# Pair products on one core: 31 rows of sixteen by difference, three TensorE turns a tile, ScalarE's queue for the head loads and the last two stores

## The chip, the cores and the metric

The kernel runs on one core of one Trainium2 chip. The metric is the device time of one execution in microseconds (us). Before the change it is 1284.42 us, the median of 3 runs that lie between 1284.36 and 1284.61.

## The reference

For 4096 batch rows, 32 fields and an embedding of 64, every pair of fields i < j is multiplied, the second field after a product with the 64x64 matrix W:

```python
vid = jnp.einsum('bfd,de->bfe', x, W)          # x: (4096, 32, 64)
idx_i, idx_j = jnp.triu_indices(32, k=1)       # 496 pairs
return x[:, idx_i, :] * vid[:, idx_j, :]       # (4096, 496, 64), float32
```

The input has 33.6 MB, the output 520 MB.

## The kernel before

The host lays the embedding (64) of two halves of the batch on the 128 partitions and cuts the rest of the batch into 16 tiles of 128 rows. A field of a tile is thus 128 partitions x 128 floats, called a unit below (512 bytes on a partition, 64 KB in all). A tile has 32 units of input and 496 units of output. The memory `mem` has 446 units; inputs and results share it.

For each tile TensorE multiplies eight blocks of four fields by `w2` (W twice on a diagonal) into the eight banks of `vid`, which fill the PSUM. VectorE multiplies fields of `mem` by fields of `vid`, one instruction for many pairs (line 247), and writes the results into `mem`. `SLOTS` is a table of 68 pieces of the output in order, each with its length in units and its place in `mem`; slot k is stored by one DMA, here called s0 to s67, when its last product is done (line 259). A slot's place is that of older slots or of spent inputs, so the first product into it waits until the store that still reads there has landed. `CUTS` are further points at which a product is split.

All DMAs are issued by SyncE, so all are in SP's queue, in program order. `HEAD` are the loads at the start: half of tile 0 (`x0`), `w`, and 176 units more in three DMAs. Two `STRETCHES` of 160 units, tiles 6 to 10 and 11 to 15, are loaded behind slots 24 and 45 (`LOAD_BEHIND`), three DMAs each. After each group of loads the next store is held until the last load but one has landed (`held`). A DMA of 128 partitions is 128 rows, one for each partition, so that each of the 16 DMA engines moves eight rows of it.

ScalarE computes nothing: it waits for loads and for VectorE's reads of the banks and then lets TensorE go with the semaphore `go`, once for each half of the banks, so twice a tile. `by_block` orders the pairs of a tile: the pairs within fields 0 to 15, the 16x16 between the halves, and the pairs within fields 16 to 31. At the end SyncE waits for the last stores, clears the semaphores and waits for s67.

Of the kernel before, what the change touches and what calls it, by code (L numbers as in the profile page):

```python
# [12 lines left out]
P = 128  # L13
# [13 lines left out]
HEAD = range(6), [(302, 128), (0, 32), (430, 16)]  # L27
STRETCHES = [
    (range(6, 11), [(286, 128), (414, 16), (430, 16)]),
    (range(11, 16), [(32, 128), (16, 16), (0, 16)]),  # L30
]

# [12 lines left out]
]  # L45
CUTS = {
    3: (46,), 6: (24,), 11: (64,), 17: (110,), 21: (6,), 28: (24,), 36: (112,), 40: (120,),
    47: (14,), 52: (30,), 53: (24,), 54: (16,), 55: (30,), 57: (48,), 59: (112,), 61: (32,),
    64: (112,), 65: (118,), 66: (32,),
}  # L50
LOAD_BEHIND = [24, 45]
# [6 lines left out]
def by_block():  # L58


    def within(lo):
        yield "step", lo, 2, 1, 0
        for k in range(2):
            yield "step", lo, 4, 2, k
        for i in (lo, lo + 8):
            yield "row", i + 4, i, 4, 4
        yield "row", lo + 8, lo, 8, 8

    yield from within(0)
    yield "row", 16, 0, 16, 16  # L70
    yield from within(16)


def products(at, ends):


    for kind, a, b, c, d in by_block():
        if kind == "row":
            rows, n, i0, di, j0, dj = c, d, b, 0, a, 1
        else:  # L80
            rows, n, i0, di, j0, dj = 16 // b, c, a, b, a + c + d, b
        r = k = 0
        while r < rows:
            room = ends[bisect_right(ends, at)] - at
            if k or room < n:
                m, w = 1, min(n - k, room)
            else:
                m, w = min(rows - r, room // n), n
            yield at, m, w, i0 + r * di + k, di, j0 + r * dj, dj
            at += m * w  # L90
            if k + w == n:
                r, k = r + m, 0
            else:
                k += w


HALF = F // 2
# [20 lines left out]

def build(nc, x0, x, w, out):
# [16 lines left out]
    seen_sp = set()  # L136
    sp_dve = 0

    def sp_wait_dve(n):
        nonlocal sp_dve  # L140
        if n > sp_dve:
            nc.sync.wait_ge(dve, n)  # L142
            sp_dve = n

    def sp_wait(s):
        if s.num not in seen_sp:
            nc.sync.wait_ge(s, 16)
            seen_sp.add(s.num)

    def load(dst, src, name, fields):  # L150
        s = sem(name)
        nc.sync.dma_start(dst, src).then_inc(s, 16)  # L152
        for t, f in fields:
            loaded[t, f] = s
        return s


    load(mem[:, PLACE[0] : PLACE[0] + HALF, :], x0[:, :HALF, :], "x0", [(0, f) for f in range(HALF)])
    ws = load(w2, w, "w", [])

    at = 0

    def stretch(tiles, runs, name):
        nonlocal at
        made = []
        for r, (lo, n) in enumerate(runs):
            for k in track.stores(lo, lo + n):
                sp_wait(stored[k])
            sp_wait_dve(track.reads(lo, lo + n))
            made.append(load(mem[:, lo : lo + n, :], x[:, at : at + n, :], f"{name}{r}", fields(tiles, lo, n)))  # L170
            for u in range(lo, lo + n):
                track.store[u] = None
                track.read[u] = 0
            at += n
        return made

    held = stretch(*HEAD, "h")[-2]

    for tiles, first, step in WALKS:
        with nc.tensor.Fori(0, len(tiles)) as k:
            for b in range(F // BANK):
                if b % (HALF // BANK) == 0:
                    nc.tensor.wait_ge(go, 1)
                    nc.tensor.sem_inc(go, -1)  # L186
                nc.tensor.matmul(  # L187
                    vid[:, b * BANK : b * BANK + BANK, :],
                    lhsT=w2,
                    rhs=mem[:, bass.ds(k * step + (first + b * BANK), BANK), :],  # L190
                    start=True,
                    stop=True,
                ).then_inc(pe, 1)
# [3 lines left out]
    rank = {}  # L197
    done = 0
    bank_read = [0] * (F // BANK)
    seen_act, seen_dve = set(), set()  # L200
    act_dve = dve_pe = dve_dve = 0
# [4 lines left out]
    for t in range(NT):  # L206
        place = PLACE[t]
        for b in range(0, F // BANK, HALF // BANK):
            for s in [ws, *(loaded[t, f] for f in range(b * BANK, b * BANK + HALF))]:
                if s.num not in seen_act:  # L210
                    nc.scalar.wait_ge(s, 16)
                    seen_act.add(s.num)
            read = max(bank_read[b : b + HALF // BANK])
            if read > act_dve:
                nc.scalar.wait_ge(dve, read)
                act_dve = read
            nc.scalar.sem_inc(go, 1)

        xt = mem[:, place : place + F, :]
        for pos, m, n, i, di, j, dj in products(t * NP, ends):  # L220
            begin = STARTS[slot]
            size, lo = SLOTS[slot]
            u = lo + pos - begin
            o = mem[:, u : u + m * n, :]
            if m == 1:
                left = xt[:, i : i + n, :]
                right = vid[:, j : j + 1, :].to_broadcast([P, n, C])
            else:
                o = o.rearrange("p (m w) c -> p m w c", m=m)
                right = vid[:, j : j + (m - 1) * dj + 1 : dj, :].unsqueeze(2).to_broadcast([P, m, n, C])  # L230
                if di == 0:
                    left = xt[:, i : i + n, :].unsqueeze(1).to_broadcast([P, m, n, C])
                else:
                    left = xt.rearrange("p (m d) c -> p m d c", d=di)[:, i // di : i // di + m, i % di : i % di + n, :]
            last = j + (m - 1) * dj
            need = t * (F // BANK) + last // BANK + 1
            if need > dve_pe:
                nc.vector.wait_ge(pe, need)
                dve_pe = need
            for s in track.stores(u, u + m * n):  # L240
                if s not in seen_dve:
                    nc.vector.wait_ge(stored[s], 16)  # L242
                    seen_dve.add(s)
            if track.reads(u, u + m * n) > dve_dve:
                dve_dve = track.reads(u, u + m * n)
                nc.vector.wait_ge(dve, dve_dve)  # L246
            nc.vector.tensor_tensor(o, left, right, MULT).then_inc(dve, 1)  # L247
            done += 1
            for r in range(m):
                for f in range(i + r * di, i + r * di + n):  # L250
                    track.read[place + f] = done
                bank_read[(j + r * dj) // BANK] = done
            if pos + m * n == begin + size:
                if held is not None:
                    sp_wait(held)
                    held = None
                sp_wait_dve(done)
                s = sem(f"s{slot}")
                nc.sync.dma_start(out[:, begin : begin + size, :], mem[:, lo : lo + size, :]).then_inc(s, 16)  # L259
                stored.append(s)  # L260
                for u in range(lo, lo + size):
                    track.store[u] = slot
                slot += 1
                if waiting and waiting[0] == slot:
                    waiting.pop(0)
                    held = stretch(*stretches.pop(0), f"g{slot}_")[-2]
# [3 lines left out]
    for k, s in enumerate(landed):  # L270
        if k not in seen_dve:
            sp_wait(s)
    numbers = sorted(s.num for s in sems)
    assert numbers == list(range(numbers[0], numbers[-1] + 1)) and final.num == numbers[-1]
    nc.sync.sem_clear(range(numbers[0], numbers[-1]))
# [4 lines left out]
def pairs():  # L280
    for _, m, n, i, di, j, dj in products(0, [NP]):
        for r in range(m):
            for k in range(n):
                yield i + r * di + k, j + r * dj
# [34 lines left out]
```

## Time and profile before

| | |
|---|---|
| median of 3 runs | 1284.42 us |
| the profiled execution: time, span | 1284.54 us, 1283.2 us |
| VectorE (DVE) busy | 1080.3 us, 292 products |
| TensorE busy, weight loads | 182.4 us, 71.2 us |
| DMA queue q1 | 99.9% of 16 engines over the span |
| DMA bytes | 33.62 MB read from HBM, 520.09 MB written, 432 GB/s |
| granted TensorE clock, mean | 0.567 |

The shares of the busy time are of the whole span. For the DMA the share is the time that packets took, as a part of what 16 engines have in the span. The profiled execution is 0.12 us above the median of the runs.

### The profile page before, as it was taken

To read this page: it belongs to the slowest core of one execution; us is meant where nothing else is said; L and a number is where in the kernel's file an instruction comes from. 1 tells how busy PE (TensorE), PEld (TensorE's weight loads), DVE (VectorE), ACT (ScalarE), POOL (GpSimd) and SP (SyncE) were. 2 spreads that over 40 slices of the span, in tenths; PEclk is the share of its full clock that TensorE was granted. 3 is DMA by queue.
4 is the path that set the end of the run, shared out by engine and by line. 5 is a ranking of instruction groups with operands and counts; after the bars stand their busy time and mean duration, and the time that the engine had idled before them with its cause. 6 is when DMAs were issued, how large, how long until landed. Compare 5 with 4: busy or idle time off the path is not lost.

```text
span 1283.2 us, 1172 instructions
## 1 busy us (share of the span) xinstructions
PE 182.4 (14%) x256; PEld 71.2 (6%) x256; DVE 1080.3 (84%) x292; POOL 0.2 (0%) x4
## 2 busy tenths in 40 slices
PE   4011040304020021021111201002112030111000
PEld 1000010101000010000000000000001010000000
DVE  5798999999996556989999998483898999899971
POOL 0000000000000000000000000000000000000000
PEclk7656565755555565555565656556556565665555
DMA  9999999999999999999999999999999999999999
GB/s 415 424 441 437 426 440 429 437 421 439 445 427 433 417 437 445 423 443 421 435 424 447 442 427 417 435 419 453 427 433 425 454 429 425 425 444 437 427 425 409
DMA packets 11380, 553.75 MB, mean 432 GB/s; under 512 B 1264, under 2 KB 1392, under 8 KB 1392
## 3 DMA queue, kind: packets, MB, share of 16 engines
q1 hardware_dynamic: 11376, 553.72, 99.9%
q14 instruction: 4, 0.03, 0.0%
HBM read 33.62 MB, written 520.09 MB: 432 GB/s over the span
## 4 chain that ended last, share of the span: by engine, by line
DVE 50%; DMA 40%; another core or an unknown queue 4%; issue 3%; SPq 0%; DVEq 0%
DVE mem L247 50%; DMA out_dram<-mem 38%; DMA mem<-in_r_x_dram 2%; SPq L152 0%; SPq L259 0%; DVEq L242 0%; SPq L142 0%; DVEq L246 0%
## 5 line engine op out<-in xcount | busy, mean ns | idle before, releaser
L247 DVE TENSOR_TENSOR mem<-mem,vid 128x1024 f32<-128x1024 f32 (+11 forms) x292 | 1080.3, 3771 | 175.4 <-DMA out_dram<-mem 144.1
L187 PE MATMUL vid<-mem,w 128*128 (+1 forms) x256 | 182.4, 880 | 1002.4 <-PEq L186 1002.4
L187 PEld LDWEIGHTS vid<-mem,w 128*128 128x128 f32 x256 | 71.2, 292 | 1112.7 <-issue 1112.7
L292 POOL MEMSET const-bfloat16-1.0<- 128x1 bf16 x1 | 0.1, 102 | 0.0
L292 POOL MEMSET const-uint8-127<- 128x1 uint8 x1 | 0.1, 102 | 0.0
L292 POOL MEMSET const-float32-0.0<- 128x1 f32 x1 | 0.1, 99 | 0.2 <-issue 0.2
L292 POOL MEMSET const-float32-1.0<- 128x1 f32 x1 | 0.1, 99 | 0.0
## 6 DMA issues: line engine op xcount, KB each, us to landing
out_dram<-mem SPq DMA_DIRECT2D x12, 7680.0 KB, 29.1
out_dram<-mem SPq DMA_DIRECT2D x11, 7168.0 KB, 23.2
out_dram<-mem SPq DMA_DIRECT2D x8, 6656.0 KB, 21.8
out_dram<-mem SPq DMA_DIRECT2D x4, 6144.0 KB, 24.1
out_dram<-mem SPq DMA_DIRECT2D x2, 5120.0 KB, 20.5
mem<-in_r_x_dram SPq DMA_DIRECT2D x6, 1024.0 KB, 57.3
out_dram<-mem SPq DMA_DIRECT2D x1, 3072.0 KB, 20.5
mem<-in_r_x_dram SPq DMA_DIRECT2D x1, 2048.0 KB, 28.1
```

Of the source, the lines that this page charges most:

```text
L187: nc.tensor.matmul(vid[:, b * BANK : b * BANK + BANK, :], lhsT=w2, rhs=mem[:, bass.ds(k * step + (first + b * BANK), BANK), :], start=True ...
L247: nc.vector.tensor_tensor(o, left, right, MULT).then_inc(dve, 1)
L292: nc = _bacc.Bacc("TRN2", target_bir_lowering=False, num_devices=1, dynamic_dma_scratch_size=256)
```

## The change

The pairs of a tile are ordered anew. Block `size` (16, 8, 4, 2, 1) has `size` rows, one for each difference d = 1 to `size`, and each row has sixteen pairs in `F // (2*size)` groups: fields i = 2*size*g to 2*size*g + size - 1 with j = F - 2*size + (i within its group) + d. So a tile is 31 rows of sixteen; one product takes m whole rows, and its second operand is a set of overlapping windows of `vid`. Products are split at fewer places: 149 products in place of 292. Of them none has fewer than 2048 floats a partition.

TensorE goes three times a tile, over banks 0 to 3, 4 and 5, 6 and 7 (`TURNS`). Tile 0 is loaded as a whole; the head loads are 160 units more, in two DMAs, and each stretch is two DMAs; 76 DMAs in place of 79, with the same bytes. ScalarE issues the head loads, so these are in its queue, and the first store waits for none of them. In a stretch the held store now waits for TensorE's first matmul of the first tile that was loaded. The last two stores, s66 and s67, are issued by ScalarE too (`SP_SLOTS`), and ScalarE waits for the stores at the end and clears the semaphores; SyncE waits for s67. `Products.emit` puts a wait on an earlier product where one product would have two. `SLOTS`, `CUTS` and `LOAD_BEHIND` have new numbers; the last three slots are (128, 176), (128, 48), (112, 176), so that s67's place is within that of s65.

```diff
-HEAD = range(6), [(302, 128), (0, 32), (430, 16)]
+HEAD = range(1, 6), [(318, 128), (0, 32)]
 STRETCHES = [
-    (range(6, 11), [(286, 128), (414, 16), (430, 16)]),
-    (range(11, 16), [(32, 128), (16, 16), (0, 16)]),
+    (range(6, 11), [(286, 128), (414, 32)]),
+    (range(11, 16), [(32, 128), (0, 32)]),
 ]
...
-    (128, 176), (128, 310), (128, 64), (128, 192), (128, 32), (120, 320),
...
+    (128, 176), (112, 64), (128, 304), (128, 176), (128, 48), (112, 176),
...
-LOAD_BEHIND = [24, 45]
+LOAD_BEHIND = [25, 46]
+SP_SLOTS = len(SLOTS) - 2
+TURNS = [(0, 4), (4, 6), (6, 8)]
...
+BLOCKS = [16, 8, 4, 2, 1]
+ROW = F // 2
 def products(at, ends):
...
+    for size in BLOCKS:
+        r = 0
+        while r < size:
+            m, over = divmod(ends[bisect_right(ends, at)] - at, ROW)
+            m = min(size - r, m)
+            yield at, size, r, m
+            at += m * ROW
+            r += m
...
-    load(mem[:, PLACE[0] : PLACE[0] + HALF, :], x0[:, :HALF, :], "x0", [(0, f) for f in range(HALF)])
-    ws = load(w2, w, "w", [])
+    sp, act = Queue(nc.sync, dve), Queue(nc.scalar, dve)
+    load(act, mem[:, a : a + F, :], x0[:, :F, :], "x0", [(0, f) for f in range(F)])
+    ws = load(act, w2, w, "w", [])
-    held = stretch(*HEAD, "h")[-2]
+    stretch(act, *HEAD, "h")
+    held = None
...
-            for b in range(F // BANK):
-                if b % (HALF // BANK) == 0:
-                    nc.tensor.wait_ge(go, 1)
-                    nc.tensor.sem_inc(go, -1)
+            for lo, hi in TURNS:
+                nc.tensor.wait_ge(go, 1)
+                nc.tensor.sem_inc(go, -1)
+                for b in range(lo, hi):
...
+            row = [groups, size * C]
+            o = mem[:, u : u + m * ROW, :].rearrange("p (m g b) c -> p m g (b c)", m=m, g=groups)
+            j = F - 2 * size + r + 1
+            right = bass.AP(vid.tensor, j * C, [[F * C, P], [C, m], [0, groups], [1, size * C]])
...
                 if held is not None:
-                    sp_wait(held)
+                    nc.sync.wait_ge(*held)
                     held = None
-                sp_wait_dve(done)
+                q = sp if slot < SP_SLOTS else act
+                q.after_products(done)
                 s = sem(f"s{slot}")
-                nc.sync.dma_start(out[:, begin : begin + size, :], mem[:, lo : lo + size, :]).then_inc(s, 16)
+                q.engine.dma_start(out[:, begin : begin + n, :], mem[:, lo : lo + n, :]).then_inc(s, 16)
...
-                    held = stretch(*stretches.pop(0), f"g{slot}_")[-2]
+                    tiles, runs = stretches.pop(0)
+                    stretch(sp, tiles, runs, f"g{slot}_")
+                    held = pe, tiles[0] * (F // BANK) + 1
...
-    nc.sync.sem_clear(range(numbers[0], numbers[-1]))
+    nc.scalar.sem_clear(range(numbers[0], numbers[-1]))
     nc.sync.wait_ge(final, 16)
```

In the built programs the change shows as follows. A row is a line, the instruction, its operands and their size a partition, and in brackets what it waits for: `s65` is the landing of store s65, `dve` a count of finished products, `pe` a count of finished matmuls.

SyncE at the end of the program before, the last twelve stores and the end:

```order
L259 DMA out_0_dram<-mem 128x14336 [waits dve]
L259 DMA out_0_dram<-mem 128x16384 [waits dve]
L259 DMA out_0_dram<-mem 128x12288 [waits dve]
L259 DMA out_0_dram<-mem 128x16384 [waits dve] x2
L259 DMA out_0_dram<-mem 128x14336 [waits dve]
L259 DMA out_0_dram<-mem 128x16384 [waits dve] x5
L259 DMA out_0_dram<-mem 128x15360 [waits dve]
L275 ISA [waits s66,s65]
```

ScalarE after the change, its whole program but for the waits and increments between the loads and the stores (before, it has no such instruction):

```order
L183 DMA mem<-in_r_x_0_dram 128x4096 [waits barrier_Pool_Activation_PE_DVE_SP_release]
L183 DMA w2<-in_L0_rec_W_dram 128x128
L183 DMA mem<-in_r_x_dram 128x16384
L183 DMA mem<-in_r_x_dram 128x4096
L292 DMA out_0_dram<-mem 128x16384 [waits w,x0,h0,dve,h1,g25_0,g25_1,g46_0,g46_1]
L292 DMA out_0_dram<-mem 128x14336 [waits dve]
L310 ISA [waits s64,s66,s43,s22]
```

So the four loads of the head and s66 and s67 have moved from SP's queue to ScalarE's; SyncE ends with s65, of 16384 floats a partition.

VectorE at the end before, the products of the last four slots and a little ahead of them:

```order
L247 TENSOR_TENSOR mem<-mem,vid 128x2048 [waits s62]
L247 TENSOR_TENSOR mem<-mem,vid 128x14336 [waits pe]
L247 TENSOR_TENSOR mem<-mem,vid 128x768
L247 TENSOR_TENSOR mem<-mem,vid 128x1280 [waits s63]
L247 TENSOR_TENSOR mem<-mem,vid 128x4096 [waits dve,pe]
L247 TENSOR_TENSOR mem<-mem,vid 128x12288 [waits s64,pe]
L247 TENSOR_TENSOR mem<-mem,vid 128x1024 x3
L247 TENSOR_TENSOR mem<-mem,vid 128x2048 x2
L247 TENSOR_TENSOR mem<-mem,vid 128x8192
```

and after the change, slots 63 to 67:

```order
L158 TENSOR_TENSOR mem<-mem,vid 128x8192
L158 TENSOR_TENSOR mem<-mem,vid 128x4096
L158 TENSOR_TENSOR mem<-mem,vid 128x2048 [waits pe]
L158 TENSOR_TENSOR mem<-mem,vid 128x16384 [waits s61]
L158 TENSOR_TENSOR mem<-mem,vid 128x16384 [waits s62,pe]
L158 TENSOR_TENSOR mem<-mem,vid 128x16384 [waits s63]
L158 TENSOR_TENSOR mem<-mem,vid 128x8192 [waits s65]
L158 TENSOR_TENSOR mem<-mem,vid 128x4096
L158 TENSOR_TENSOR mem<-mem,vid 128x2048
```

The last slot waited for s64 before and waits for s65 now; s64, s65 and s66 are one product each, and they wait for s61, s62 and s63.

SyncE around the loads of the first stretch before:

```order
L259 DMA out_0_dram<-mem 128x15360 [waits dve]
L259 DMA out_0_dram<-mem 128x16384 [waits dve]
L152 DMA mem<-in_r_x_dram 128x16384 [waits s21,s18]
L152 DMA mem<-in_r_x_dram 128x2048 x2
L259 DMA out_0_dram<-mem 128x14336 [waits dve,g24_1]
L259 DMA out_0_dram<-mem 128x16384 [waits dve] x2
```

and after the change:

```order
L292 DMA out_0_dram<-mem 128x16384 [waits dve] x4
L292 DMA out_0_dram<-mem 128x14336 [waits dve]
L183 DMA mem<-in_r_x_dram 128x16384 [waits s22]
L183 DMA mem<-in_r_x_dram 128x4096
L292 DMA out_0_dram<-mem 128x16384 [waits dve,pe]
L292 DMA out_0_dram<-mem 128x14336 [waits dve]
```

The load behind the first is one of 4096 floats a partition in place of two of 2048, and the store behind them waits for a matmul in place of the middle load.

More of the change, by code (lines that the diff above doesn't have):

```diff
@@ L26 @@
 PLACE = [first + step * k for tiles, first, step in WALKS for k in range(len(tiles))]
-HEAD = range(6), [(302, 128), (0, 32), (430, 16)]
+HEAD = range(1, 6), [(318, 128), (0, 32)]
 STRETCHES = [
-    (range(6, 11), [(286, 128), (414, 16), (430, 16)]),
-    (range(11, 16), [(32, 128), (16, 16), (0, 16)]),
+    (range(6, 11), [(286, 128), (414, 32)]),
+    (range(11, 16), [(32, 128), (0, 32)]),
 ]
+FRESH = [0] + [tiles[0] for tiles, _ in STRETCHES]
 SLOTS = [
[9 rows of a table removed]
[9 rows of a table added]
 ]
 CUTS = {
-    3: (46,), 6: (24,), 11: (64,), 17: (110,), 21: (6,), 28: (24,), 36: (112,), 40: (120,),
-    47: (14,), 52: (30,), 53: (24,), 54: (16,), 55: (30,), 57: (48,), 59: (112,), 61: (32,),
-    64: (112,), 65: (118,), 66: (32,),
-}
-LOAD_BEHIND = [24, 45]
[3 rows of a table added]
+}
+LOAD_BEHIND = [25, 46]
+SP_SLOTS = len(SLOTS) - 2
+TURNS = [(0, 4), (4, 6), (6, 8)]
 PAD = 24
@@ L55 @@
 STARTS = [0, *accumulate(n for n, _ in SLOTS)]
[L58 to L71, printed above, removed]
-def products(at, ends):
[L77 to L97, printed above, removed]
+BLOCKS = [16, 8, 4, 2, 1]
+ROW = F // 2
+def products(at, ends):
+    for size in BLOCKS:
[3 more added lines that the diff above has]
+            m = min(size - r, m)
+            assert m, (at, over)
+            yield at, size, r, m
+            at += m * ROW
+            r += m
 def fields(tiles, lo, n):
@@ L116, in reads, with __init__, after_products, after @@
         return max(self.read[lo:hi])
+class Queue:
+    def __init__(self, engine, dve):
+        self.engine, self.dve = engine, dve
+        self.seen, self.products = set(), 0
+    def after_products(self, n):
+        if n > self.products:
+            self.engine.wait_ge(self.dve, n)
+            self.products = n
+    def after(self, s, known_to_product=None):
+        if s.num not in self.seen and not (known_to_product and known_to_product <= self.products):
+            self.engine.wait_ge(s, 16)
+        self.seen.add(s.num)
+class Products:
+    def __init__(self, engine, pe, dve):
+        self.engine, self.pe, self.dve = engine, pe, dve
+        self.steps = []
+    def add(self, waits, earliest, *operands):
+        self.steps.append((waits, earliest, operands))
+    def emit(self):
+        waits = [dict(w) for w, _, _ in self.steps]
+        for k, (_, earliest, _) in enumerate(self.steps):
+            w = waits[k]
+            for s in (self.pe, self.dve):
+                if len(w) < 2 or s not in w:
+                    continue
+                first = earliest if s is self.pe else w[s]
+                for b in range(k - 1, max(k - 6, first - 1), -1):
+                    if not waits[b]:
+                        waits[b][s] = w.pop(s)
+                        break
+        seen = {}
+        for w, (_, _, operands) in zip(waits, self.steps):
+            for s, n in w.items():
+                if n > seen.get(s.num, 0):
+                    self.engine.wait_ge(s, n)
+                    seen[s.num] = n
+            self.engine.tensor_tensor(*operands, MULT).then_inc(self.dve, 1)
 def build(nc, x0, x, w, out):
@@ L135, in build, with load @@
     stored = []
[L136 to L150, printed above, removed]
+    sp, act = Queue(nc.sync, dve), Queue(nc.scalar, dve)
+    def load(q, dst, src, name, fields):
         s = sem(name)
-        nc.sync.dma_start(dst, src).then_inc(s, 16)
+        q.engine.dma_start(dst, src).then_inc(s, 16)
         for t, f in fields:
@@ L155, in load, with stretch @@
         return s
-    load(mem[:, PLACE[0] : PLACE[0] + HALF, :], x0[:, :HALF, :], "x0", [(0, f) for f in range(HALF)])
-    ws = load(w2, w, "w", [])
+    a = PLACE[0]
+    load(act, mem[:, a : a + F, :], x0[:, :F, :], "x0", [(0, f) for f in range(F)])
+    ws = load(act, w2, w, "w", [])
     at = 0
-    def stretch(tiles, runs, name):
+    first_read = {}
+    def stretch(q, tiles, runs, name):
         nonlocal at
@@ L166, in stretch @@
         for r, (lo, n) in enumerate(runs):
+            q.after_products(track.reads(lo, lo + n))
             for k in track.stores(lo, lo + n):
-                sp_wait(stored[k])
-            sp_wait_dve(track.reads(lo, lo + n))
-            made.append(load(mem[:, lo : lo + n, :], x[:, at : at + n, :], f"{name}{r}", fields(tiles, lo, n)))
+                q.after(stored[k], first_read.get(k))
+            made.append(load(q, mem[:, lo : lo + n, :], x[:, at : at + n, :], f"{name}{r}", fields(tiles, lo, n)))
             for u in range(lo, lo + n):
@@ L175, in stretch @@
         return made
-    held = stretch(*HEAD, "h")[-2]
+    stretch(act, *HEAD, "h")
+    held = None
     for tiles, first, step in WALKS:
         with nc.tensor.Fori(0, len(tiles)) as k:
-            for b in range(F // BANK):
-                if b % (HALF // BANK) == 0:
-                    nc.tensor.wait_ge(go, 1)
[L186 to L193, printed above, removed]
+            for lo, hi in TURNS:
+                nc.tensor.wait_ge(go, 1)
+                nc.tensor.sem_inc(go, -1)
+                for b in range(lo, hi):
+                    nc.tensor.matmul(
+                        vid[:, b * BANK : b * BANK + BANK, :],
+                        lhsT=w2,
+                        rhs=mem[:, bass.ds(k * step + (first + b * BANK), BANK), :],
+                        start=True,
+                        stop=True,
+                    ).then_inc(pe, 1)
     ends = sorted({*STARTS, *(STARTS[k] + c for k, cuts in CUTS.items() for c in cuts)})
-    rank = {}
+    vector = Products(nc.vector, pe, dve)
     done = 0
     bank_read = [0] * (F // BANK)
-    seen_act, seen_dve = set(), set()
-    act_dve = dve_pe = dve_dve = 0
+    turned = [0] * (F // BANK)
+    dve_pe = dve_dve = 0
     slot = 0
@@ L207, in build @@
         place = PLACE[t]
[L208 to L216, printed above, removed]
+        for lo, hi in TURNS:
+            for s in [ws, *(loaded[t, f] for f in range(lo * BANK, hi * BANK))]:
+                act.after(s)
+            act.after_products(max(bank_read[lo:hi]))
+            turned[lo:hi] = [act.products] * (hi - lo)
@@ L217, in build @@
             nc.scalar.sem_inc(go, 1)
-        xt = mem[:, place : place + F, :]
-        for pos, m, n, i, di, j, dj in products(t * NP, ends):
+        start = done
+        for pos, size, r, m in products(t * NP, ends):
             begin = STARTS[slot]
-            size, lo = SLOTS[slot]
+            n, lo = SLOTS[slot]
             u = lo + pos - begin
[L224 to L236, printed above, removed]
-            if need > dve_pe:
[L238 to L247, printed above, removed]
-            done += 1
[L249 to L253, printed above, removed]
@@ new lines, in build @@
+            groups = F // (2 * size)
+            row = [groups, size * C]
+            o = mem[:, u : u + m * ROW, :].rearrange("p (m g b) c -> p m g (b c)", m=m, g=groups)
+            left = mem[:, place : place + F, :].rearrange("p (g h) c -> p g (h c)", g=groups)
+            left = left[:, :, : size * C].unsqueeze(1).to_broadcast([P, m, *row])
+            j = F - 2 * size + r + 1
+            right = bass.AP(vid.tensor, j * C, [[F * C, P], [C, m], [0, groups], [1, size * C]])
+            top = j + m + size - 2
@@ new lines, in build @@
+            waits = {}
+            need = t * (F // BANK) + top // BANK + 1
+            if need > dve_pe:
+                waits[pe] = dve_pe = need
+                dve_dve = max(dve_dve, turned[top // BANK])
+            for s in track.stores(u, u + m * ROW):
+                if s not in first_read:
+                    waits[stored[s]] = 16
+                    first_read[s] = done + 1
+            if track.reads(u, u + m * ROW) > dve_dve:
+                waits[dve] = dve_dve = track.reads(u, u + m * ROW)
@@ L254, in build @@
+            early = t not in FRESH and top < TURNS[-1][0] * BANK
+            vector.add(waits, max(start - 2, turned[top // BANK]) if early else start, o, left, right)
+            done += 1
+            for g in range(groups):
+                for f in range(size):
+                    track.read[place + 2 * size * g + f] = done
+            for b in range(j // BANK, top // BANK + 1):
+                bank_read[b] = done
+            if pos + m * ROW == begin + n:
                 if held is not None:
-                    sp_wait(held)
+                    nc.sync.wait_ge(*held)
@@ L256, in build @@
                     held = None
-                sp_wait_dve(done)
+                q = sp if slot < SP_SLOTS else act
+                q.after_products(done)
                 s = sem(f"s{slot}")
-                nc.sync.dma_start(out[:, begin : begin + size, :], mem[:, lo : lo + size, :]).then_inc(s, 16)
+                q.engine.dma_start(out[:, begin : begin + n, :], mem[:, lo : lo + n, :]).then_inc(s, 16)
                 stored.append(s)
-                for u in range(lo, lo + size):
+                for u in range(lo, lo + n):
@@ L265, in build @@
                     waiting.pop(0)
-                    held = stretch(*stretches.pop(0), f"g{slot}_")[-2]
+                    tiles, runs = stretches.pop(0)
+                    stretch(sp, tiles, runs, f"g{slot}_")
+                    held = pe, tiles[0] * (F // BANK) + 1
+    vector.emit()
     *landed, final = stored
     for k, s in enumerate(landed):
-        if k not in seen_dve:
-            sp_wait(s)
+        act.after(s, first_read.get(k))
     numbers = sorted(s.num for s in sems)
     assert numbers == list(range(numbers[0], numbers[-1] + 1)) and final.num == numbers[-1]
-    nc.sync.sem_clear(range(numbers[0], numbers[-1]))
+    nc.scalar.sem_clear(range(numbers[0], numbers[-1]))
     nc.sync.wait_ge(final, 16)
@@ L280, in pairs @@
 def pairs():
[L281 to L284, printed above, removed]
+    for _, size, r, m in products(0, [NP]):
+        for d in range(r + 1, r + m + 1):
+            for g in range(F // (2 * size)):
+                for i in range(size):
+                    yield 2 * size * g + i, F - 2 * size + i + d
 _INS = ["r_x", "L0_rec_W"]
@@ L296 @@
     x = x.reshape(2, NT, C, F, D).transpose(0, 4, 1, 3, 2).reshape(P, NT, F, C)
-    x0 = _np.pad(x[:, 0, :HALF], ((0, 0), (0, PAD0), (0, 0)))
+    x0 = _np.pad(x[:, 0], ((0, 0), (0, PAD0), (0, 0)))
     order = [t * F + f for tiles, runs in (HEAD, *STRETCHES) for lo, n in runs for t, f in fields(tiles, lo, n)]
```

19 rows, old and new, of tables (CUTS, SLOTS) are left out of this document.

## The prediction

> **What bounds the kernel now.** I read the page's head first, then its DMA queues, then the chain of work, then stretches of the span.
>
> ```profile
> span 1283.2 us, 1172 instructions
> PE 182.4 (14%) x256; PEld 71.2 (6%) x256; DVE 1080.3 (84%) x292; POOL 0.2 (0%) x4
> DMA  9999999999999999999999999999999999999999
> q1 hardware_dynamic: 11376, 553.72, 99.9%
> q14 instruction: 4, 0.03, 0.0%
> HBM read 33.62 MB, written 520.09 MB: 432 GB/s over the span
> DVE 50%; DMA 40%; another core or an unknown queue 4%; issue 3%; SPq 0%; DVEq 0%
> ```
>
> The chain gives VectorE half of the span, which invites the conclusion that fewer and longer products must help. The queue row denies it: the 16 DMA engines hold packets for 99.9% of the span, and no slice is below nine tenths. VectorE stands beside that and waits for memory to be stored:
>
> ```profile
> DVE mem L247 <- DMA out_dram<-mem: 144.1, 31, 20.2
> ```
>
> So the time is the bytes over the rate of the DMA engines, plus what the engines stand idle. The next rows have the columns: length of the stretch, busy us of each engine, granted clock, share of the DMA engines and GB/s.
>
> ```profile
> 31.00:440.00 409.00, 58.31 (x81) 22.37 (x79) 367.61 (x99) 0.00 (x0) 0.56 1.01 435
> 440.00:500.00 60.00, 9.58 (x16) 3.89 (x16) 33.62 (x13) 0.00 (x0) 0.56 0.98 419
> 840.00:900.00 60.00, 8.73 (x16) 3.60 (x16) 33.50 (x16) 0.00 (x0) 0.59 0.98 421
> 900.00:1250.00 350.00, 47.43 (x64) 18.48 (x64) 318.35 (x89) 0.00 (x0) 0.56 1.00 434
> ```
>
> A stretch of stores runs at 434 to 435 GB/s; about the two groups of loads it is 419 and 421. At 434.5 GB/s a store of 128 units (8.39 MB) takes 19.3 us, one of 112 units 16.9 us, and one of its eight rows on each engine 2.41 us. The bytes stay the same, so a gain can come only from the few us outside this, and a loss from any moment at which the queues run dry. That is what each part is priced by.
>
> **Fewer products, new order of pairs.** The forms that remain, line engine op, shapes, count, busy us and mean ns:
>
> ```profile
> L247 DVE TENSOR_TENSOR mem<-mem,vid 128x16384 f32<-128x16384 f32 x3 | 51.7, 17220 | 5.7 <-DMA out_dram<-mem 3.0 <-issue 2.7
> L247 DVE TENSOR_TENSOR mem<-mem,vid 128x8192 f32<-128x8192 f32 x26 | 225.7, 8680 | 1.3 <-DMA out_dram<-mem 1.3
> L247 DVE TENSOR_TENSOR mem<-mem,vid 128x4096 f32<-128x4096 f32 x5 | 22.1, 4412 | 0.0
> L247 DVE TENSOR_TENSOR mem<-mem,vid 128x2048 f32<-128x2048 f32 x77 | 173.1, 2280 | 21.4 <-DMA out_dram<-mem 21.4
> ```
>
> From 2048 to 16384 floats the time rises by 14.94 us for 14336 floats, 1.042 ns each; the rest, 0.15 us, is paid once a product. 143 products fewer are at most 21 us of VectorE. On the path this is worth nothing: it lengthens the 144.1 us in which VectorE waits for stores. The overlapping windows as an operand are in no row. If they cost nothing, nothing changes; they decide once a slot of 128 units takes longer than its store, 19.3 against 17.22 us, so from 12% more a float. The forms above, whose operands repeat fields too, lie on one line whatever their shape, so I take nothing, and leave a small chance for it.
>
> **Head.** Columns are start, length, engine and instructions; the last row is of the chain.
>
> ```profile
> 6.37 6.58 PE L187 MATMUL vid<-mem,w 128*128 x8 [6.37 <-PEq L186]
> 12.98 31.58 DVE L247 TENSOR_TENSOR mem<-mem,vid 128x1024 f32<-128x1024 f32 x7 [12.98 <-PE vid L187]
> 2.11 28.15 DMA mem<-in_r_x_dram
> ```
>
> Tile 0 as a whole is 1 MB more before TensorE can begin, 2.4 us, so 8.8 us; the first product needs fields up to 19, five matmuls at 0.82 us in place of eight, and begins at about 13 us as before. Slot 0 is a product of 8192 and one of 4096 floats, 13.1 us, and is ready at 26. The loads run until about 31 us, so its store finds the engines busy: nothing, with 5 us of cover. Loads and store then overlap, whichever queue goes first; the loads there are wanted by tile 5. With the cover gone, a late first store would cost its lateness.
>
> **Three turns of TensorE; hold and loads of a stretch.** Turns cost two more signals a tile at most, on an engine that is busy 14%. The hold is on SP's queue, with every later store behind it.
>
> ```profile
> 468.03 0.50 PEld L187 LDWEIGHTS vid<-mem,w 128*128 128x128 f32 x2 [94.61 <-issue]
> 469.05 0.34 PEld L187 LDWEIGHTS vid<-mem,w 128*128 128x128 f32 x1 [0.52 <-issue]
> 470.17 5.64 SPq L259 DMA_DIRECT2D out_dram<-mem  x2
> 474.22 3.48 DVE L247 TENSOR_TENSOR mem<-mem,vid 128x1024 f32<-128x1024 f32 x3 [9.61 <-PE vid L187]
> ```
>
> Before, the store is issued at 470.17 with one load of 1 MB, 2.4 us, still to move, and the engines stay at 0.98. After, it is issued when the first matmul is done, about 1.5 us after 468.03, and from the first load's landing (467.7: the middle one's at 470.17 less 2.4) 2 MB, 4.8 us, are still to move, to 472.5: 3.0 us of cover in place of 2.4. VectorE waits there 9.61 us for TensorE, so its reads of the banks are over in time. Nothing; if VectorE were late by more than 3 us, the engines would stand for the rest. The three transfers fewer can save part of what the stretches lose: 60 us x (1 - 419/434.5) = 2.1 us each, most of it the turn from stores to loads, which stays. Between 0 and 2.1 us I take 0.3, since only one of several transfers goes.
>
> **The last two stores on the other queue.** This is the part that can cost. Let 0 be when the engines finish the last row of s63. In one queue s64 moves from 0 to 19.3, s65 to 38.6, s66 to 57.9 and s67 to 74.8 us. Two delays come from stretches at both ends:
>
> ```profile
> 0.00:2.00 2.00, 0.00 (x0) 0.00 (x0) 0.00 (x0) 0.20 (x4) 1.00 0.23 37
> 1282.00:1283.20 1.20, 0.00 (x0) 0.00 (x0) 0.00 (x0) 0.00 (x0) 0.50 0.00 0
> 0.73 0.38 SPq L152 DMA_DIRECT2D mem<-in_r_x_dram  x1
> ```
>
> The engines are busy 0.46 us of the first 2, so from 1.54 at the latest to about 1.75 us: 1.0 us after the issue at 0.73. Behind the last row 1.2 us pass until the end is signalled. s62 then has landed at -16.9 + 1.2 = -15.7, and s65's product ends 17.22 us later at 1.5. s63 has landed at 1.2, so s66's product runs from 1.5 to 18.7, and its first row could move at 19.8. At that moment s65, in SP's queue, has just begun its first row.
>
> Now two queues have rows for the same engines for the first time. Priced from both sides: if the engines finish s65 first, s65 lands at 39.8, the three products of s67 (8680 + 4412 + 2280 ns = 15.37 us) end at 55.2 and its rows are there at 56.2, 1.7 us before s66 is through: nothing. If the engines take a row from each in turn, s65 has had k = 1 row alone, and its last ends at 19.3 + 2.41 + 7 x 4.82 = 55.4. It lands at 56.6, the products of s67 end at 72.0 and its rows come at 73.1; s66 is through at 57.9. The engines stand for 15.2 us, and nothing else is left to move. In general the gap is 17.6 - 2.41 k: 17.6 where s66 comes first, 12.8 with k = 2. A gain has no place here: the bytes are the same and s67 cannot come earlier than in one queue.
>
> Which end? Before, q1 is the only queue with stores, so no row shows two such queues. The nearest is q14, which brings instructions:
>
> ```profile
> 1195.37 30.93 DMA out_dram<-mem
> out_dram<-mem SPq DMA_DIRECT2D x1, 33.2
> q1 hardware_dynamic: 1, 0.07, 34.7%
> q14 instruction: 1, 0.01, 3.9%
> ```
>
> The first row ends at 1226.30 with a store landing; the second is the next store, issued in the stretch 1212 to 1213 and landed 33.2 us later, near 1246. Its eight rows move in between. The last two rows are what started from 1232.5 to 1233.0: a packet of q14 and a row of q1. So in the middle of a transfer, with rows of q1 waiting, the engine gave a packet to the other queue and then went on. That is nearest to the second end, and I take 15.2 us.
>
> The Trainium skill, "DMA: Bandwidth & Descriptors", section "Queues, rings and completion order", says that each engine goes round the queue rows that have work, a packet at a time; the q14 packet agrees, and the sum by it is the one just made. The same place gives a packet as some 9 to 17 descriptors, and here a transfer has eight rows and one signal on each engine; taken so, an engine would finish its share of s65 before it turned to s66, and the sum would be without the 15.2 us. The q14 packet stood inside a share, which speaks against this reading, by one packet.
>
> **The sum.** 1284.54 us for the profiled execution (1.34 us of it outside the span), - 0.3 for the loads, + 15.2 for the gap: 1299.4; the median of the runs is 0.12 lower, so 1299.3 us.
>
> **The rivals.**
> A, the forecast: row about between the queues. k from 0 to 2 and 0 to 2.1 us for the loads: 1295 to 1302 us.
> B, not slower: the queues are served share by share or in order of arrival, and s65 is through before s66. It decides at s65's landing: as long as that is not over 1.7 us later than at 39.8, nothing stands. For it is that q1's rows before come strictly in order; against it the q14 packet. 1284.54 - 0.3 - 0.12 = 1284.1, with 2.1 us or nothing off: 1282.3 to 1284.6.
> C, VectorE's windows cost over 12%: each further per cent of 1080 us is about 10 us, beside or without the gap: over 1302. Nothing in the forms speaks for it.
> D, faster by over 0.2%: both stretches lose their 2.1 us and B holds: below 1281.9.
>
> **How the numbers follow.** 0.2% is 2.6 us, about what a measurement of this kernel can tell from no change. A has 0.65: one kind of packet shows the turn, though an instruction queue may have a right of its own. B has 0.27. C has 0.05, D 0.03. Faster 0.03, same 0.26, slower 0.71 (A, C and a rest of B). A's own range is 1295 to 1302. To leave out no more than 2 in 10 the range must take in most of B: 1283.4 to 1302.
>
> **What the next profile would show.** If A holds: DMA share of 9 in all slices but the last, which falls; VectorE with one wait of some 38 us for a store near the end, before three products; s65 and s66 landing within 3 us of each other, each about 38 us after s65 began; a gap of 13 to 18 us before s67's rows. If B holds, s66 lands 19 us after s65 and the share stays at 9. VectorE's busy time should fall by 10 to 21 us to 1059 to 1070 without a change of the total; stops at 480 or 880 us would show the hold as wrong. The prediction is wrong if the engines do not turn from row to row, or if s67 is late for another reason.

## The result, and the profile after

The changed kernel takes 1299.64 us (median of 4 runs, 1299.44 to 1300.32) against 1284.51 us before (4 runs beside it). The ratio is 1.0118, with a 95% interval of 1.0105 to 1.0131: 1.2% slower. The forecast was 1299.3 us.

The page's head and its DMA queues, after:

```profile
span 1297.7 us, 1043 instructions
PE 201.8 (16%) x256; PEld 71.7 (6%) x256; DVE 1070.7 (83%) x149; POOL 0.2 (0%) x4
DMA  9999999999999999999999999999999999999995
q1 hardware_dynamic: 10080, 525.34, 93.7%
q10 hardware_dynamic: 864, 28.38, 5.1%
HBM read 33.62 MB, written 520.09 MB: 427 GB/s over the span
```

The bytes are the same. A second queue, q10, has appeared: it is ScalarE's. Of 40 slices only the last is not full. The end in order of time (start, length, engine, instructions, in brackets the idle time ahead and what ended it), and then three stretches of it (length, busy us of PE, PEld, DVE, POOL, clock, DMA share, GB/s). In these views and in the queue rows below, a packet counts wholly in the stretch in which it starts, so a share can be over 1:

```profile
1191.70 34.35 DVE L158 TENSOR_TENSOR mem<-mem,vid 128x16384 f32<-128x16384 f32 x2 [0.95 <-DMA out_dram<-mem]
1226.08 53.58 ACTq L292 DMA_DIRECT2D out_dram<-mem  x2
1264.06 15.21 DVE L158 TENSOR_TENSOR mem<-mem,vid 128x8192 f32<-128x8192 f32 x3 [38.01 <-DMA out_dram<-mem]
```

```profile
1226.50:1265.50 39.00, 0.00 (x0) 0.00 (x0) 1.44 (x1) 0.00 (x0) 0.50 0.99 430
1266.00:1280.00 14.00, 0.00 (x0) 0.00 (x0) 13.28 (x3) 0.00 (x0) 0.50 0.00 0
1280.00:1297.70 17.70, 0.00 (x0) 0.00 (x0) 0.00 (x0) 0.00 (x0) 0.50 0.96 415
```

VectorE finishes s66's product, then waits 38.01 us for s65 to land, makes the last slot in 15.21 us, and in the stretch of 14 us that holds these products the DMA engines move nothing. Summed from the packets in the trace, the 16 engines stand for 14.5 us on average there (the texts recorded before the experiments say 14.4); the two spans differ by 14.5.

What each queue moved tells why. The rows are those of the two queues in four stretches, with packets, MB and share: 1226.5 to 1231.5, to 1260.5, to 1263, to 1265 us (16 packets of 0.00 MB are the signals of one transfer, one from each engine; a row of 64 KB from each engine is 1.05 MB):

```profile
q1 hardware_dynamic: 48, 2.10, 97.3%
...
q10 hardware_dynamic: 96, 6.29, 50.1%
q1 hardware_dynamic: 96, 6.29, 50.1%
...
q10 hardware_dynamic: 16, 1.05, 96.9%
...
q10 hardware_dynamic: 16, 1.05, 121.0%
q1 hardware_dynamic: 16, 0.00, 0.5%
```

First q1 alone has two rows of s65 an engine (and s64's signals). Then each queue has six, at 50.1% each. By the starts of the packets these are a row of s66, then a row of s65 and so on, six times over, on all 16 engines: they take the rows in turn. Then one row of s66, and only with the eighth row of s66 the signals of s65.

### The profile page after: what moved, and what is told of

Same layout as the page of the kernel before. It is cut to its first block, busy times and chain, and to the rows that moved or that the text cites. A ratio compares the mean times of both kernels' runs of the same rounds, so it can differ in the third digit from the quotient of the medians.

```text
span 1297.7 us, 1043 instructions
## 1 busy us (share of the span) xinstructions
PE 201.8 (16%) x256; PEld 71.7 (6%) x256; DVE 1070.7 (83%) x149; POOL 0.2 (0%) x4
## 4 chain that ended last, share of the span: by engine, by line
DVE 56%; DMA 28%; another core or an unknown queue 11%; issue 2%; PE 2%; ACTq 0%; DVEq 0%
DVE mem L158 56%; DMA out_dram<-mem 27%; PE vid L223 2%; DMA w<-in_L_rec_W_dram 1%; ACTq L183 0%; ACTq L249 0%; DVEq L156 0%
## 5 line engine op out<-in xcount | busy, mean ns | idle before, releaser
L158 DVE TENSOR_TENSOR mem<-mem,vid 128x2048 f32<-128x2048 f32 (+7 forms) x149 | 1070.7, 7249 | 208.5 <-DMA out_dram<-mem 157.6
L223 PE MATMUL vid<-mem,w 128*128 (+1 forms) x256 | 201.8, 950 | 975.9 <-PEq L221 764.3
```

The lines of the kernel that those rows point to most:

```text
L158: self.engine.tensor_tensor(*operands, MULT).then_inc(self.dve, 1)
L223: nc.tensor.matmul(vid[:, b * BANK : b * BANK + BANK, :], lhsT=w2, rhs=mem[:, bass.ds(k * step + (first + b * BANK), BANK), :], start=True ...
```

## Experiments

The theory of the prediction, A: the engines take turns between the two queues row by row, so s65 lands with s66 and not 19 us ahead of it, and the products that wait for s65 find nothing left to cover them. Its rivals, beside B of the prediction: the new order, turns or head cost something (R); a second queue is itself slower (Q); the queues share by bytes (Y).

| run | median us, runs | ratio to before, 95% | engines stand at the end, us |
|---|---|---|---|
| changed kernel | 1299.64, 4 | 1.0118 [1.0105, 1.0131] | 14.5 |
| all stores on SyncE | 1285.47, 10 | 1.0006 [0.9997, 1.0016] | 0 |
| s67 in s64's place | 1285.56, 10 | 1.0007 [0.9997, 1.0017] | 0 |
| three stores on ScalarE | 1285.27, 8 | 1.0004 [0.9994, 1.0015] | 0 |
| a wait for s65 ahead of s66 | 1286.75, 8 | 1.0014 [1.0004, 1.0025] | 2.0 |
| s66 in quarters | 1286.97, 8 | 1.0019 [1.0007, 1.0030] | 1.9 |
| s65 in quarters | 1302.07, 2 | 1.0136 [1.0107, 1.0166] | 17.0 |
| before, two stores on ScalarE | 1285.04, 8 | 1.0001 [0.9989, 1.0012] | 0 |
| the same, s67 in s65's place | 1285.94, 8 | 1.0011 [0.9999, 1.0022] | 1.9 |
| the same, s66 in quarters | 1284.86, 8 | 0.9994 [0.9980, 1.0008] | 0.2 |

The last column is worked out from starts and lengths of the packets, as the mean time of the 16 engines without one between the last row ahead of s67 and the first of s67 (for the wait: ahead of s66). The ratio is to the kernel before, run anew beside each group of runs (medians 1284.80 to 1284.88 us beside the experiments).

**All stores on SyncE.** The edit; the waits for the stores at the end and the clearing of the semaphores are moved to SyncE too:

```diff
-SP_SLOTS = len(SLOTS) - 2
+SP_SLOTS = len(SLOTS)
```

> s66 and s67 go back to SyncE's queue, which also clears the semaphores; everything else of the change stays (order of pairs, three turns, head loads on ScalarE). Theory A (s65 and s66 share the engines row by row, so s65 lands late and s67's products wait): the gap of 14.4 us is gone, 1284.5 to 1285.4 us, s66 lands 19 us after s65. Rival R (the new order of the pairs, the turns or the head cost something): it stays above 1286.5 us.

The span on that run's page, and its end in order of time:

```profile
span 1283.6 us, 1042 instructions
```

```profile
1190.82 71.97 SPq L292 DMA_DIRECT2D out_dram<-mem  x4
1247.21 15.22 DVE L158 TENSOR_TENSOR mem<-mem,vid 128x8192 f32<-128x8192 f32 x3 [21.12 <-DMA out_dram<-mem]
```

s65 lands at 1247.2 in place of 1264.0 and the 14.5 us are gone. The order of the pairs, the turns, the head on ScalarE and the new hold are all still there, so R falls as the cause of the loss. The median is 0.07 us above the expected range and 0.7 us above the kernel before, which the ratio does not tell from nothing (1.0006, 0.9997 to 1.0016). But 0.5 of the 0.7 lies outside the span, and that part is clear: 1.80 to 1.88 us in these ten runs, 1.28 to 1.37 in the 31 of the kernel before beside them. Which part of the change makes it was not tested.

**The last slot in s64's place.**

```diff
-    (128, 176), (112, 64), (128, 304), (128, 176), (128, 48), (112, 176),
+    (128, 176), (112, 64), (128, 304), (128, 176), (128, 48), (112, 304),
```

> The last slot is put where s64 stood, (112, 304) in place of (112, 176), and nothing else: s66 and s67 stay in ScalarE's queue. Theory A: s65 and s66 still share the engines and land within 3 us of each other, but nothing waits for s65, so no gap: 1284.5 to 1285.4 us. Rival Q (a second queue is itself slower, whoever waits): still 1299 to 1300 us.

```profile
1226.84 17.38 ACTq L292 DMA_DIRECT2D out_dram<-mem  x2
1228.62 15.22 DVE L158 TENSOR_TENSOR mem<-mem,vid 128x8192 f32<-128x8192 f32 x3 [1.81 <-DMA out_dram<-mem]
```

The stores stay on ScalarE and still share: s65 landed at 1264.8 and s66 at 1267.3 us. But the products wait 1.81 us for s64 and not 38 us for s65, and the engines stand for nothing. The median is 0.16 us above the expected range and not told from the kernel before. So sharing costs nothing that can be measured by itself; what costs is that something waits for the store whose landing it delays. Q falls.

**Three stores on ScalarE.**

```diff
-SP_SLOTS = len(SLOTS) - 2
+SP_SLOTS = len(SLOTS) - 3
```

> One store more on ScalarE: s65, s66 and s67. s65 and s66 are then in one queue in order, and s64 and s65 share the engines. Theory A: s64 and s65 land within 3 us of each other, but only s65 is waited for and s66's 19.3 us still lie behind it, against 15.2 us of products and 2 us of delays: a gap of 0 to 1.5 us, 1284.5 to 1287 us. Rival Q (each store on the second queue costs): 1299 us or more.

```profile
1247.51 15.22 DVE L158 TENSOR_TENSOR mem<-mem,vid 128x8192 f32<-128x8192 f32 x3 [21.13 <-DMA out_dram<-mem]
```

One store more on the second queue, and the loss is gone, since s65 and s66 are in one queue again. s64 now shares with s65 and lands at 1242.6 in place of 1227.9 us; nobody waits for it. One expectation missed: s64 and s65 land 4.9 us apart and not within 3, since s64 had three rows alone, where s65 has two in the changed kernel.

**A wait for s65 ahead of s66.** ScalarE waits until s65 has landed before it issues s66:

```diff
                 q.after_products(done)
+                if slot == SP_SLOTS:
+                    q.after(stored[-1])
```

> ScalarE waits for s65's landing before it issues s66: one wait more. Theory A: the queues never hold rows at the same time, so s65 lands some 17 us earlier; the engines stand once for a landing and an issue, 1.8 to 2.4 us: 1286.3 to 1288 us. Rival Q: the wait comes on top of 1299.6, 1301 us or more.

It was 1286.75 us: a wait more makes the kernel 13 us faster than the changed one, and the 2.0 us for which the engines stand are the landing of s65 and the issue of s66.

**s66 in quarters, s65 in quarters.** The store is issued as four DMAs of 32 units in the same queue, once for s66 and once for s65, where the products of s67 then wait for all four parts:

```diff
-                q.engine.dma_start(out[:, begin : begin + n, :], mem[:, lo : lo + n, :]).then_inc(s, 16)
+                cut = n // 4 if slot == SPLIT else n
+                for p in range(0, n - cut, cut):
+                    part = sems[-1]
+                    parts.append(part)
+                    q.engine.dma_start(out[:, begin + p : begin + p + cut, :], mem[:, lo + p : lo + p + cut, :]).then_inc(part, 16)
+                    s = sem(f"s{slot}_{p}")
+                p = n - cut
+                q.engine.dma_start(out[:, begin + p : begin + n, :], mem[:, lo + p : lo + n, :]).then_inc(s, 16)
```

> s66 is stored as four DMAs of 32 units, so its rows are a quarter as long (16 KB, 0.61 us); same bytes, same queue, ScalarE. Theory A, turns by row: s65's rows then wait 0.61 us for each of s66's, s65 is through about 23 us after its first row in place of 34, and s66 has 15 us left: a gap of 1 to 3.5 us, 1286 to 1289 us. Rival Y, the queues share by bytes: the gap stays at 14.4 us, 1299 to 1300 us.

> The mirror: s65 is stored as four DMAs of 32 units, s66 whole. Theory A, turns by row: s66's eight long rows stand between eight short ones of s65, s66 is through first, and the rest of s65 moves alone; when s65 lands nothing is left: the whole chain of landing, products and issue is gap, 16.5 to 18 us, 1301.5 to 1303.5 us. Rival Y, by bytes: 14.4 us as in the changed kernel, 1299 to 1300 us.

The wait for s65 ahead of the last products, with s66 in quarters and with s65 in quarters:

```profile
1252.13 15.22 DVE L159 TENSOR_TENSOR mem<-mem,vid 128x8192 f32<-128x8192 f32 x3 [25.39 <-DMA out_dram<-mem]
```

```profile
1267.09 15.21 DVE L159 TENSOR_TENSOR mem<-mem,vid 128x8192 f32<-128x8192 f32 x3 [40.57 <-DMA out_dram<-mem]
```

The same bytes in the same queues: with short rows in s66 the wait falls from 38 to 25 us and 1.9 us of gap are left, with short rows in s65 it rises to 41 and the gap to 17.0. Y, sharing by bytes, would have left it as it was in both. The packets show the same directly: in the first run each of s65's last six rows of 64 KB stands behind one row of 16 KB of s66, in the second one short row of s65, or one of its signals, stands between two long rows of s66. The turn is by row, whatever its length.

**The kernel before with two stores on ScalarE**, and the same with s67 in s65's place. The first has the first edit alone (SyncE clears the semaphores when s67 has landed), the second both:

```diff
-                sp_wait_dve(done)
+                q = nc.sync
+                if slot < len(SLOTS) - 2:
+                    sp_wait_dve(done)
+                else:
+                    q = nc.scalar
+                    q.wait_ge(dve, done)
...
-    (128, 176), (128, 310), (128, 64), (128, 192), (128, 32), (120, 320),
+    (128, 176), (128, 310), (128, 64), (128, 192), (128, 32), (120, 192),
```

> The kernel before, with s66 and s67 issued by ScalarE and nothing else (SyncE clears the semaphores after s67 has landed). There s67 waits for s64. Theory A: s65 and s66 share the engines for as many rows as s65 has left, nothing waits for s65, no gap: 1284.3 to 1285 us. Rival Q: over 1290 us.

> The run before, and s67's place moved into s65's (120, 192): the one ingredient that it lacked. Before, s66 was issued at 1239.4 us, when s65 had five or six rows behind it. Theory A: s65's last two or three rows are spread over twice the time, it lands 4.8 to 9 us later than in one queue, and the products of 120 units (17 us) no longer fit: a gap of 2 to 8 us, 1286 to 1293 us; much less than 14.4 since k is larger. Rival Z, the gap is there whenever both ingredients are, of the same size: 1298 us or more. Rival B, no turns: 1284 to 1285.5 us.

The first costs nothing (1285.04 us, 0.04 above the expected range, and not told from before), as A has it, but no rows were shared there: all rows of s65 went ahead of the first of s66, only s65's signals came behind one of them, and nothing waits for s65. The second took 1285.94 us, 0.06 below what A expected, and by its ratio (0.9999 to 1.0022) the time alone is not told from no change; its trace shows 1.9 us of gap, but not by the way that was expected. The queues' rows there, from 1239 to 1244.2, to 1246.4 and to 1249 us:

```profile
q1 hardware_dynamic: 32, 2.10, 93.3%
...
q10 hardware_dynamic: 16, 1.05, 110.1%
...
q10 hardware_dynamic: 16, 1.05, 93.0%
q1 hardware_dynamic: 16, 0.00, 0.3%
```

ScalarE issued s66 at 1239.1, and a store alone reaches the engines in some 0.9 us; but s65's last two rows went ahead, so there was no turn of rows at all. s65's rows were through at 1244.3 us on the first engines and at 1245.4 on the last, and yet its signals went out behind a row of s66, and it landed at 1248.3. That is 4.0 us after the first engine's last row, as the next expectation counts it, and 2.9 us after the last engine's, which is the one that the landing waits for. That alone made the 1.9 us of gap. So a new question: does the signal wait its turn, or are the writes slow when another queue is busy?

**The same with s66 in quarters**, cut as above:

> The run before it with both ingredients (the old kernel, s67 in s65's place, s66 and s67 on ScalarE), and s66 as four DMAs with rows of 16 KB. In the run before all rows of s65 were through before the first of s66, and yet s65 landed 4 us later and 1.9 us of gap stood. Theory T (the signal that tells the landing is a packet of its own and waits its turn behind a row of the other queue, 2.42 us there): it now waits 0.61 us, s65 lands about 1.8 us earlier after its last row, the gap shrinks to 0 to 0.4 us, 1284.3 to 1285.4 us. Rival W (the writes of s65 themselves finish late while another queue is busy): the landing stays at 3 to 4 us behind the last row and the gap at 1.9 us, 1285.6 to 1286.8 us.

The stretches 1239 to 1244.2 and 1244.2 to 1246.4 us of that run:

```profile
q1 hardware_dynamic: 29, 1.90, 84.6%
q10 hardware_dynamic: 14, 0.23, 10.3%
...
q10 hardware_dynamic: 57, 0.93, 99.4%
q1 hardware_dynamic: 16, 0.00, 0.4%
```

The signals now go out before 1246.4, behind a row of 16 KB; s65 landed at 1246.3, 1.1 us after the last engine's last row in place of 2.9, and the gap fell from 1.9 to 0.2 us. The signal waits its turn. W, slow writes, falls by the packets: from the start of an engine's signal to its landing 0.3 to 0.5 us pass, in this run, in the run before it, in the changed kernel (s65) and for a store that shares with nobody (s64 in the changed kernel). What is longer is the time ahead of the signal. In the changed kernel, too, s65 landed 2.9 us after the last engine's last row, 2.4 of them a row of s66.

## Why the prediction was right, point by point

**What bounds it.** Right: VectorE's busy time fell from 1080.3 to 1070.7 us and nothing came of it. The fall is 9.6 us, just under the 10 to 21 foreseen: 143 products at 0.067 and not 0.15 us, since most products start some 0.08 us before the one ahead of them has ended (255 of the 292 before). The windows cost nothing:

```profile
L158 DVE TENSOR_TENSOR mem<-mem,vid 128x8192 f32<-128x8192 f32 x20 | 173.4, 8680 | 57.2 <-DMA out_dram<-mem 40.6 <-PE vid L223 16.6
```

A product of 8192 floats takes 8680 ns as before, so rival C falls.

**The last two stores.** The step that carried the forecast, the turn from row to row read off one instruction packet, held in each run in which both queues had rows for long (the changed kernel, s67 in s64's place, three stores on ScalarE, both runs with quarters); rival B falls, in both of its forms. The Trainium skill, "DMA: Bandwidth & Descriptors", section "Queues, rings and completion order", has the engines go round the queues a packet at a time; the 96 and 96 packets agree, if one row of 64 KB is a packet. Its 9 to 17 descriptors to a packet do not fit these transfers, if a row is a descriptor: the turn came after every row.

The size came out at 14.5 for 15.2 us, but by luck: two errors nearly cancel. The term k, rows that s65 has alone, was 2 and not 1: s66's first row came 5.7 us after its issue, behind a second row of s65, where the prediction allowed 1.1. By the prediction's 17.6 - 2.41 k that would have been 12.8 us. And from s65's last row on the slowest engine to its landing 2.9 us passed and not 1.2, by the signal's turn, which no step had. The 1.2 was misread besides: it comes from a stretch in which no row starts, but two engines move rows until 1282.8 us there, so in one queue it is 0.4. The products took 15.21 for 15.37 us.

The total, 1299.64 for 1299.3 us, is close by luck as well. The gap is 0.7 us less than forecast; 0.3 us for the loads did not come off, and 0.4 us were added outside the span, which the sum took over as 1.34 us and which is 1.74 in the profiled execution of the changed kernel. Of the 15.1 us between the medians the idle engines make 14.5.

**Loads.** The 0.3 us for three transfers fewer did not show: with all stores on SyncE the span is 1283.6 us, before 1283.2. Nor were there 2.1 us a stretch to save. If each packet counts by the part of it that lies within, the stretches from 440 and 840 us move 427 and 428 GB/s before, against 433 to 434 in the longer ones around them, which is less than 1 us each; after the change they move 426 and 426.

**The head** cost nothing, but with less cover than the prediction had:

```profile
9.47 9.62 PE L223 MATMUL vid<-mem,w 128*128 x16 [9.47 <-ACTq L249]
16.55 25.88 DVE L158 TENSOR_TENSOR mem<-mem,vid 128x8192 f32<-128x8192 f32 x3 [16.55 <-PE vid L223]
29.60 0.37 SPq L292 DMA_DIRECT2D out_dram<-mem  x1
```

The first product began at 16.55 and not 13, and the first store came at 29.60 and not 26. A block of four fields is two entries of MATMUL in the trace (256 for 128 blocks), so the eight of before were half a tile and not a whole one, and the first product waits for ten entries. Of 5 us of cover 2 were left: the loads moved until about 31.6 us on most engines, s0's first row came as they ended, and the engines did not stand.

**The hold** failed by the same reading, without a price that can be measured:

```profile
482.47 8.65 PE L223 MATMUL vid<-mem,w 128*128 x16 [95.70 <-ACTq L249]
484.57 18.19 SPq L292 DMA_DIRECT2D out_dram<-mem  x2
```

The store comes 2.1 us after TensorE begins and not 1.5, and the 3.0 us of cover were not there: the engines stood for 0.2 us in the changed kernel and for 0.0 to 0.9 in the other runs with this hold (0.7 with s67 in s64's place). At the second stretch they stood for less than 0.1.

## What to carry to other kernels

Where the DMA engines are full, as here, a second queue brought no bandwidth but took away the order: a store that landed 19 us ahead of its neighbour in one queue landed 2.4 us ahead of it in two. Before a transfer is moved to another queue, ask which work waits for the one that it will share with, and how much is then left to move while that work is done. If nothing waits, the move is free; if something does, keep both in one queue, wait for another buffer, or make the rows of the one that nobody waits for short.

## What the runs showed of the hardware that was not expected

- The signal of a finished transfer is a packet of its own in its queue and waits for its turn. Behind a row of 64 KB of the other queue a store landed 2.9 us after the last engine's last row (in the changed kernel, and in the kernel before with both edits), behind a row of 16 KB 1.1 us after it; in one queue it was 0.5 us (s64 in the changed kernel).
- A newly issued store does not get the next turn. In the changed kernel its first row came 5.7 us after the issue, against 0.9 us for a store that found the engines free (s67). If it takes these 0.9 us to arrive, one or two more rows of 64 KB of the other queue went first, behind the one that was moving; with s65 in rows of 16 KB it was five or six rows, 4.3 us after the issue. So it is no fixed count of rows, and what an engine holds ahead was not found out.
- The turn costs no rate: 434 GB/s from 1231.5 to 1260.5 us, where the rows of two queues alternate, and 434 with one queue.
